# Where the last batch keeps its held tiles, and the order of the last change between layers

## The chip, the cores and the metric

The kernel runs on one core of a Trainium2 chip. The metric is the device time of one execution in microseconds (us); three executions of the kernel before gave 3567.22, 3568.37 and 3571.44 us, median 3568.37 us. The core's engines are TensorE (PE, matmuls; its weight loads are listed apart as PEld), VectorE (DVE), ScalarE (ACT), GpSimd (POOL), and SyncE (SP), which here does nothing but issue DMAs. Each engine takes its instructions in the order in which the kernel writes them, and waits on the others by semaphores.

## The reference

Two layers over 8 batches of 2048 nodes with 256 features, in fp32. Layer 0 is attention in chunks of 256 keys, each chunk with a softmax of its own, with two layer norms behind it; layer 1 is graph attention with an `elu`, and again a layer norm.

```
# layer 0, heads of 64 features
scores = clip(einsum("bhnd,bhjcd->bhnjc", q, kc) / 8, -10, 10)
scores = where(mask == 0, -10, scores)
attn   = softmax(scores, axis=-1)              # over each chunk of 256 keys
ctx    = einsum("bhnjc,bhjcd->bhnd", attn, vc) # sums the 8 chunks
x1     = layernorm(x + layernorm(ctx @ Wo.T + bo + x) * gamma + beta)
...
# layer 1
Wh     = x1 @ W
e      = leaky_relu(s_src[i] + s_dst[j], 0.2)  # masked by adj
h_out  = elu(softmax_j(e) @ Wh)
x      = layernorm(x1 + h_out)
```

## The kernel before

**Layer 0** of a batch goes in 64 slots, two to a pair, so 32 pairs. A slot is one group of 512 query nodes, one pair of heads and one chunk of keys. For each pair PE writes four score tiles (`unit`, line 424) into PSUM, DVE masks and clips each into an SBUF tile `pr` of 128x1024 (`evict`, line 441), ACT takes the exponential in place (`exps`, line 464), and PE multiplies two `pr` tiles by the values in each `product` (line 475). Scores of pair p+1 are made while the products of pair p run. PSUM gives them three rooms of two banks (`two_banks`), handed out in turn to score tiles, products and projections alike: the first product of a pair takes the room of the second score tile, the second product that of the third. The `pr` tiles come from the pool `prp` with 6 buffers, four to a pair. So the third `pr` of a pair takes the buffer of the first `pr` of the pair before, which the first product has to have read.

After each product ACT copies the result out (line 482), DVE takes reciprocals (line 492), and POOL multiplies and adds to the sum `acc` (lines 499, 501). Each group of 512 nodes, once its two `acc` are complete, goes through `Between`: `output` (line 628), `add` (639), a first norm, `scale` (645), `shift` (616), `again` (648), a second norm, `finish` (ACT applies it and issues the store to `x1D`), a turn, and `values` (670), which makes the layer 1 inputs `waug` and `sd`. For most groups this is laid over the pairs of the next group by the tables `FIRST_OF` to `NEXT_LAST`.

**Layer 1** of a batch has 128 tiles, 16 for each of 8 units (a half of the nodes and a head). `make` builds a weight tile `e` of 128x1024 on DVE (line 916) from a row, a factor and a mask tile that SP loads; `use` is 32 matmuls on it (line 947). When a unit is done, ACT copies it out (line 969) and `close` finishes it in five steps, each called by `rest`: reciprocals on DVE, a scaling, `exp` and `relu` on ACT (1006, 1007), and a last DVE operation into `h1` (1011). In the last batch alone the scaling is one POOL operation (995), else eight on ACT (1001). `Close` then adds the layer 0 result to a group of `h1`, takes its norm and stores the output; its `add`, `sums`, `squares`, `factors` and `finish` are hung on pairs by tables.

Layer 1 of batch b-1 (`lower`) runs along with layer 0 of batch b, four tiles a pair. In the last batch, b = 7, the last `LATE` = 8 slots (pairs 28 to 31) run without it; 16 tiles of batch 6 are held back for the stretch in which the last group of batch 7 goes through `Between`. The order of that stretch is written out by hand in the list `order` (from line 1387): `M` is a `make`, `U` a `use`, `R` one step of `close`, `early` the second norm and `values` of the group before, `steps` those of the last group, `fs` the factors of layer 1 (`fs[0]` begins with the greatest value over nodes, line 737). Every engine's queue follows this list. Behind it layer 1 of batch 7 runs alone (64 calls of `step`, two tiles each); there every third tile is made by ACT (885, 886) and POOL (887).

Memory around the change: in the first batch only (`spare`) half of the `pr` tiles lie in `h1`. In batch 7 the closings of groups 0 and 1 of batch 6 are spread over pairs 20 to 31 (`CLOSING_EARLY`) and load into `qT[:, 0]` and `qT[:, 1]`. The last group's input is loaded by `load_x` into the pool `blocks` at pair 31 and gets its bias in the list `order`.

Of the kernel before, what the change touches and what calls it, by code (L numbers as in the profile page):

```python
# [8 lines left out]
F32 = mybir.dt.float32  # L9
# [5 lines left out]
ALU = mybir.AluOpType  # L15
# [7 lines left out]
def adj_resnorm_kernel(  # L23
# [49 lines left out]
    FIRST = [sum(BANKS[:m]) for m in range(len(BANKS))]  # L73
    TILES = len(UNITS) * NT
    STEP = TILES // SLOTS
    LATE = 8
    WIDE = max(BANKS)
    AHEAD_E = 5
    AHEAD_P = 8
# [153 lines left out]
    class Masks:  # L233
# [57 lines left out]

        return dram[b, g * CH : (g + 1) * CH, :].rearrange("(t p) f -> p t f", p=P)

    def load_x(b, g, name):
        t = blocks.tile([P, QT, F], F32, tag="xb", name=name)
        at = by_node(x, b, g)
        post((name, b, g), nc.sync.dma_start, lambda k: t[:, k, :], lambda k: at[:, k, :])
        return t
# [105 lines left out]

    where = [(s // QS, s % QS // NK, s % NK) for s in range(SLOTS)]
    slab_of, probs, raws, accs = {}, {}, {}, {}
    spare = [1]

    def load_slab(p):
        q, hp, c = where[2 * p]  # L410
# [22 lines left out]
    def evict(s, u, ps):  # L433
        k = s % 2 * KT + u
        if spare and k >= KT:
            at = (s // 2 % 2 * KT + k - KT) * QT
            pr = h1[:, at : at + QT, :].rearrange("p (k t) f -> p k (t f)", k=2)
        else:
            pr = prp.tile([P, 2, CH], F32, tag="pr", name="pr")
        row = slab_of[s // 2][:, s % 2 * KT + u, :]  # L440
        nc.vector.scalar_tensor_tensor(  # L441
            pr,
            ps,
            -CLIP,
            row.unsqueeze(1).to_broadcast([P, 2, CH]),
            op0=ALU.max,
            op1=ALU.min,
        )
        probs.setdefault(s, []).append(pr)
# [12 lines left out]
    def exps(s, u):  # L462
        pr = probs[s][u]
        nc.scalar.activation(pr, pr, AF.Exp, scale=0.125)  # L464
# [66 lines left out]
    class Norm:  # L531
# [46 lines left out]
                    accum_out=self.mv[:, k, 1:2],  # L578
                )

        def factors(self):
            self.rs = small.tile([P, QT], F32, tag="rs", name="rs_" + self.name, bufs=3)
            self.off = small.tile([P, QT], F32, tag="off", name="off_" + self.name, bufs=3)
            nc.vector.tensor_scalar(self.rs, self.mv[:, :, 1], EPS, None, ALU.add)
            nc.vector.tensor_scalar(self.off, self.mv[:, :, 0], ROOT_F, None, ALU.mult)
            nc.gpsimd.tensor_tensor(self.rs, self.rs, nhalf, ALU.pow)
            nc.gpsimd.tensor_mul(self.off, self.off, self.rs)

# [11 lines left out]
    class Between:  # L600

        def __init__(self, b, g, sd, waug):
            self.b, self.g, self.sd, self.waug = b, g, sd, waug
            self.r = load_x(b, g, "xg")
            self.y = blocks.tile([P, QT, F], F32, tag="y", name="y")

        def bias(self):
# [184 lines left out]
    class Layer1:  # L794
        def __init__(self, b, gd, waug):
            self.b, self.gd, self.waug = b, gd, waug
            self.made = self.used = 0
            self.rows, self.edge, self.e = {}, {}, {}
            self.tail, self.held = [], []
            self.room = ep, "e"  # L800
            self.alone = b == B - 1
            self.masks = {}
            self.begun, self.lifted = 0, {}
# [86 lines left out]
        def make(self):  # L890

            if self.made == TILES:
                return
            k = self.made
            n, j = k // NT, k % NT
            _, h = UNITS[n]
            if j == (1 if self.alone else NT // 2):
                self.load_row(n + 1)
            self.made += 1
            if not self.alone:  # L900
                drip()
                if j == 0:
                    need(("row", self.b, n))
                self.load_edge(k + AHEAD_E)
                pool, tag = self.room
                e = pool.tile([P, WIDE * P], F32, tag=tag, name="e")
                row = self.rows[n]
            else:
                if j == NT // 2:
                    self.lift(n + 1)  # L910
                self.make_ahead(k)
                if self.by_pool(k):
                    return
                e = prp.tile([P, WIDE * P], F32, tag="pr", name="e")
                row = self.lifted[n]
            nc.vector.scalar_tensor_tensor(  # L916
                e,
                row,
                self.gd[:, h, j : j + 1],
                self.mask(k),  # L920
                op0=ALU.max,
                op1=ALU.mult,
            )
            self.e[k] = e

        def use(self):
# [14 lines left out]
                    ]  # L941
            e = self.e.pop(k)

            def products(e, j, tiles):
                for i in tiles:
                    for z in range(2):
                        nc.tensor.matmul(  # L947
                            self.pa[i // QT][z * D : (z + 1) * D, i % QT, :],
                            lhsT=e[:, i * P + z * D : i * P + (z + 1) * D],
                            rhs=self.waug[:, j, h, :],  # L950
                            start=(j == 0 and i % QT == 0),
                            stop=(j == NT - 1 and i % QT == QT - 1),
                            skip_group_check=True,
                        )
# [22 lines left out]
        def close(self, u, raw, pas):  # L977
# [12 lines left out]
                nc.vector.tensor_scalar(dn, raw[:, :, D:D1], 1e-30, None, ALU.max)  # L990
            nc.vector.reciprocal(dn, dn)
            yield 1
            if self.alone:
                v = raw[:, :, :D]
                nc.gpsimd.tensor_mul(v, v, dn.to_broadcast([P, n, D]))  # L995
            for k in range(n):
                if k == n // 2:
                    yield 1
                if not self.alone:
# [142 lines left out]
    for g in range(NCH):  # L1142
# [36 lines left out]
        11: [(3, "factors"), (3, "finish")],  # L1179
    }  # L1180
    CLOSING_EARLY = {
        20: [(0, "load", qT, 0)],
        22: [(0, "add"), (0, "sums")],
        23: [(0, "squares")],
        24: [(1, "load", qT, 2), (0, "factors"), (0, "finish")],
        26: [(1, "add"), (1, "sums")],
        27: [(1, "squares")],
        28: [(1, "factors")],
        31: [(1, "finish")],
    }  # L1190
    CLOSING_ALONE = {
        0: [(2, "load", kT, 2)],
# [21 lines left out]
    for b in range(B):  # L1214
# [9 lines left out]
        for p in range(PAIRS):  # L1224
            s0, s1 = 2 * p, 2 * p + 1
            q, i = p // QP, p % QP
            along = lower if b + 1 < B or s0 < SLOTS - LATE else None
            more = p + 1 < PAIRS
            slow[0] = bool(along) and more
            if not slow[0]:  # L1230
# [15 lines left out]

            ending = b + 1 == B and not more
            if ending:
                last = Between(b, NCH - 1, sd, waug)

            hook(FIRST_OF, {})
            if i == QP - 1 and q > 1:
# [14 lines left out]
            else:  # L1267
# [3 lines left out]
                if not lower and masks.left():  # L1271
                    masks.step()
            if ending:
                lower.make()
            hook(MIDDLE_OF, NEXT_MIDDLE)
            for each in closings:
# [13 lines left out]
            if along:  # L1290
                normalize(s0)
                if more:
                    for us_ps in waiting[1:]:
                        evict(*us_ps[0], us_ps[1])
            elif more:
                evict(*waiting[2][0], waiting[2][1])
                exps(*us[3])
            if i == 0 and q:
                send_context(b, q - 1, 1)
            if i == QP // 2:  # L1300
                send_context(b, q, 0)
            if along:
                if more:
                    exps(*us[2])
                along.rest(1)
                along.use()
                along.make()
                along.use()
                along.make()
                along.use()  # L1310
            elif ending:
                lower.use()
                group.again()
# [73 lines left out]
        else:  # L1387


            lower.room = prp, "pr"  # L1390
            M, U, R = lower.make, lower.use, lambda: lower.rest(1)
            order = [begin, U, U, ctx, early[0], steps[0], steps[1], early[2], steps[2]]
            order += [lambda: group.a.stats(every), before.turn_all, lambda: coming.load_masks(0)]
            order += [group_shift, M, M, U, steps[4], early[5], U, early[6], M]
            order += [steps[5], U, M, M, R, U, M, U, steps[6], R, steps[7], M, M, U, steps[8], R]
            order += [U, steps[9], M, R, M, M, U, U, R, fs[0], M, U, fs[1], M, U, fs[2], lambda: coming.start(fs[4])]
            done = sum(p is U for p in order) + 1, sum(p is M for p in order) + 1
            order += [R, M, U] * (LATE * STEP - done[0])
            assert LATE * STEP - done[0] >= LATE * STEP - 2 - done[1]
        for piece in order:  # L1400
            send()
            piece()
# [67 lines left out]
```

## Time and profile before

| what | value |
|---|---|
| time, median of 3 | 3568.37 us (3567.22 to 3571.44) |
| time of the profiled execution | 3565.6 us |
| its span, first to last instruction | 3563.7 us |
| granted TensorE clock, mean | 0.997 |
| PE busy | 3500.3 us, 98% |
| DVE busy | 3025.5 us, 85% |
| ACT busy | 2308.5 us, 65% |
| POOL busy | 1421.3 us, 40% |
| scores, line 424 | 8192 matmuls, 942.4 us |
| products, line 475 | 30720 matmuls, 980.6 us |
| layer 1 products, line 947 | 32768 matmuls, 1051.6 us |
| `evict`, line 441 | 960 x 1203 ns |
| `exps`, line 464 | 960 x 1054 ns |
| `make`, line 916, from a row in SBUF | 896 x 1334 ns |

Busy times are sums over the whole span. Where PE is busy all the time, an idle other engine costs nothing; where PE has gaps, the question is what it waits for. The page's second part cuts the span into 40 slices of 89 us each with one digit for each engine. The trace also gives an engine's instructions in order of time, each with the idle time ahead of it and what ended it, and the busy time of the engines in any stretch that one names.

### The profile page before, as it was taken

What the parts mean: (1) busy time and instruction counts of PE and PEld (TensorE: products, weight loads), DVE (VectorE), ACT (ScalarE), POOL (GpSimd) and SP (SyncE); (2) the same over time, 40 slices, a digit from 0 to 9 for tenths busy, and PEclk for the clock granted to TensorE, in tenths of its full rate; (3) what the DMA queues carried; (4) which work ended last, traced back from release to release, by engine and by line L of the source; (5) the groups of instructions that cost most, each with busy time, mean ns of one, the idle gap of its engine ahead of it and who ended that gap; (6) DMA issues with size and microseconds to landing.
All of it is one profiled execution on the core that took longest, in us unless ns stands there. A gap on an engine that the chain in (4) does not pass through costs nothing. (4 is left out here: it accounts for less than half of the span.)

```text
span 3563.7 us, 170248 instructions
## 1 busy us (share of the span) xinstructions
PE 3500.3 (98%) x76924; PEld 2607.6 (73%) x76924; DVE 3025.5 (85%) x3640; ACT 2308.5 (65%) x4151; POOL 1421.3 (40%) x1261
## 2 busy tenths in 40 slices
PE   8999999999999999999999999999999999999888
PEld 5666677777777777777777767777677776777677
DVE  5886699987999789996999969999699996999778
ACT  4787456655766666665666656666576665766677
POOL 1555233333443333333343334433343342434467
PEclk9999999999999999999999999999999999999999
DMA  7663333443434434434444434344343434444322
GB/s 178 150 133 79 85 102 102 108 101 100 115 107 109 101 111 114 110 103 91 124 110 112 104 89 123 106 111 102 96 125 109 108 94 103 126 111 114 106 86 68
DMA packets 719271, 385.53 MB, mean 108 GB/s; under 512 B 432976, under 2 KB 678608, under 8 KB 718544
## 3 DMA queue, kind: packets, MB, share of 16 engines
q1 hardware_dynamic: 668544, 340.95, 37.4%
q10 hardware_dynamic: 50000, 33.70, 3.0%
q8 instruction: 601, 9.85, 1.1%
q14 instruction: 126, 1.03, 0.1%
HBM read 317.59 MB, written 56.89 MB: 105 GB/s over the span
## 5 line engine op out<-in xcount | busy, mean ns | idle before, releaser
L464 ACT ACTIVATE pr<-pr 128x1024 f32<-128x1024 f32 x960 | 996.2, 1054 | 433.4 <-DVE pr L441 364.8
L441 DVE SCALAR_TENSOR_TENSOR pr<-ps,slab 128x1024 f32<-128x1024 f32 x960 | 1115.2, 1203 | 95.7 <-PE ps L424 83.1
L916 DVE SCALAR_TENSOR_TENSOR e<-srow,gd,et 128x1024 f32<-128x1024 f32 x896 | 1165.5, 1334 | 5.6 <-DMA srow<-rowD 0.6
L947 PEld LDWEIGHTS pa<-waug,e 128*64 128x64 f32 x32768 | 999.4, 138 | 199.9 <-issue 172.2
L947 PE MATMUL pa<-waug,e 128*64 128x65 f32 x32768 | 1051.6, 223 | 20.5 <-DVE e L916 14.1
L475 PE MATMUL pc<-vaug,pr 128*64 128x65 f32 x30720 | 980.6, 222 | 5.4 <-DVE pr L441 5.1
L499 POOL TENSOR_TENSOR part<-raw,rd 128x512 f32<-128x512 f32 x446 | 474.4, 1064 | 1224.6 <-DVE rd L492 1220.5
L475 PEld LDWEIGHTS pc<-vaug,pr 128*64 128x64 f32 x30720 | 938.0, 138 | 19.5 <-DVE pr L441 16.4
L424 PE MATMUL ps<-qT,kT 64*64 64x512 f32 x8192 | 942.4, 596 | 5.9 <-DVE pr L441 3.3
L424 PEld LDWEIGHTS ps<-qT,kT 64*64 64x64 f32 x8192 | 286.6, 132 | 483.7 <-issue 270.0
L482 ACT COPY raw<-pc 128x520 f32<-128x520 f32 x512 | 303.0, 592 | 492.7 <-PE pc L475 490.0
L501 POOL TENSOR_TENSOR acc<-acc,part 128x512 f32<-128x512 f32 x446 | 584.4, 1310 | 35.0
L492 DVE RECIPROCAL rd<-raw 128x8 f32<-128x8 f32 x512 | 100.3, 196 | 131.3 <-ACT raw L482 124.5
L499 POOL TENSOR_TENSOR acc<-raw,rd 128x512 f32<-128x512 f32 x64 | 66.9, 1046 | 353.0 <-DVE rd L492 353.0
L670 PE MATMUL pw<-w_sb,x1T 128*64 128x264 f32 (+1 forms) x800 | 124.3, 392 | 0.7 <-ACT x1T L336 0.6
L368 PE MATMUL pp<-xT,wk_sb 128*128 128x512 f32 x256 | 118.8, 604 | 2.9 <-DVE xT L324 1.6
L628 PE MATMUL po<-wo_sb,qT 128*64 128x256 f32 (+1 forms) x912 | 121.5, 382 | 0.0
L368 PE MATMUL pp<-xT,wq_sb 128*128 128x512 f32 x256 | 117.4, 598 | 0.0
L1001 ACT ACTIVATE sums<-sums,dn 128x64 f32<-128x64 f32 x448 | 117.1, 335 | 0.4 <-ACT y L591 0.4
L384 PE MATMUL pv<-wv_sb,xT 128*128 128x256 f32 x512 | 116.6, 381 | 0.0
L384 PEld LDWEIGHTS pv<-wv_sb,xT 128*128 128x128 f32 x512 | 95.9, 190 | 20.2 <-issue 7.2
L916 DVE SCALAR_TENSOR_TENSOR e<-rowp,gd,et 128x1024 f32<-128x1024 f32 x86 | 103.8, 1268 | 1.3 <-PE rowp L783 1.3
(151 smaller groups left out, 2514.0 us busy)
## 6 DMA issues: line engine op xcount, KB each, us to landing
et<-edgeD SPq DMA_DIRECT2D x896, 128.0 KB, 2.6
slab<-clipD SPq DMA_DIRECT2D x256, 256.0 KB, 3.7
srow<-rowD SPq DMA_DIRECT2D x252, 128.0 KB, 3.5
xg<-in_x_dram SPq DMA_DIRECT2D x128, 128.0 KB, 3.2
x1D<-y ACTq DMA_DIRECT2D x32, 512.0 KB, 3.0
ctxD<-acc ACTq DMA_DIRECT2D x56, 256.0 KB, 3.7
ctx<-ctxD SPq DMA_DIRECT2D x224, 64.0 KB, 2.9
xp<-in_x_dram SPq DMA_DIRECT2D x224, 64.0 KB, 2.2
```

The source lines that it names most:

```text
L368: nc.tensor.matmul(pps[c], lhsT=w[:, kc, c * P : (c + 1) * P], rhs=st["xT"][:, kc, :], start=(kc == 0), stop=(kc == KC - 1),)
L384: nc.tensor.matmul(pv[:, u, :], lhsT=st["xT"][:, kc, u * P : (u + 1) * P], rhs=wv_sb[:, kc, :], start=(kc == 0), stop=(kc == KC - 1),)
L424: nc.tensor.matmul(ps[z * D : (z + 1) * D, k, :], lhsT=kT[rows, hp, t * P + z * D : t * P + (z + 1) * D], rhs=qT[rows, hp, cols], start=Tr ...
L441: nc.vector.scalar_tensor_tensor(pr, ps, -CLIP, row.unsqueeze(1).to_broadcast([P, 2, CH]), op0=ALU.max, op1=ALU.min,)
L464: nc.scalar.activation(pr, pr, AF.Exp, scale=0.125)
L475: nc.tensor.matmul(pc[z * D : (z + 1) * D, k, to], lhsT=probs[s][u][:, k, i * P + z * D : i * P + (z + 1) * D], rhs=vaug[:, KT * c + u, 2 ...
L482: nc.scalar.copy(raws[s].rearrange("p k i d -> p k (i d)"), pc[:, :, : QT * D1])
L499: engine.tensor_mul(part, raw[:, :, :, :D], rd.to_broadcast([P, 2, QT, D]))
L501: engine.tensor_add(accv, accv, part)
L670: nc.tensor.matmul(pw[z, k, : F + 2 * H], lhsT=self.x1T[:, c, u * P + z.start : u * P + z.stop], rhs=w1_sb[:, c, :], start=(c == 0), stop= ...
L916: nc.vector.scalar_tensor_tensor(e, row, self.gd[:, h, j : j + 1], self.mask(k), op0=ALU.max, op1=ALU.mult,)
L947: nc.tensor.matmul(self.pa[i // QT][z * D : (z + 1) * D, i % QT, :], lhsT=e[:, i * P + z * D : i * P + (z + 1) * D], rhs=self.waug[:, j, h ...
```

## The change

`LATE` goes from 8 to 12, so that layer 1 of batch 6 ends its run alongside after pair 25 and 24 tiles are left for later. Room for more tiles is found in memory that is used up by then:

- from pair 26 on, the third `pr` of each pair lies by turns in `qT[:, 0, :1024]` and in the first quarter of `h1` (`lone`), not in `prp`;
- pairs 27 to 30 each call `rest` and `make` once; the first goes into `ep`, the next three into the second quarter of `h1` and two pieces of `qT` (`extra`); the views `like` and `block` fit row, mask and matmul operand to the shape of the third piece;
- the last group's input goes into `kT[:, 0]`, and its bias is added in pair 31, ahead of that pair's `make`, which now goes into `prp`.

Closings 0 and 1 of batch 6 take pairs 20 to 27 in place of 20 to 31. Units 6 and 7 of batch 6 are scaled by POOL, not by ACT. In the last list, `again` of the group before moves from pair 31 to behind `ctx`; the second norm of that group takes `sums` and `squares` on ACT and `factors` on POOL in place of `stats` on DVE; the list has 23 `U` and 17 `M` in another order, with all `U` ahead of `coming.start`.

```diff
-    LATE = 8
+    LATE = 12
...
-    spare = [1]
+    spare, lone = [1], []
...
             pr = h1[:, at : at + QT, :].rearrange("p (k t) f -> p k (t f)", k=2)
+        elif lone and k == KT:
+            pr = lone[s // 2 % 2]
         else:
...
-        def factors(self):
+        def factors(self, engine=nc.vector):
...
-            nc.vector.tensor_scalar(self.rs, self.mv[:, :, 1], EPS, None, ALU.add)
-            nc.vector.tensor_scalar(self.off, self.mv[:, :, 0], ROOT_F, None, ALU.mult)
+            engine.tensor_scalar(self.rs, self.mv[:, :, 1], EPS, None, ALU.add)
+            engine.tensor_scalar(self.off, self.mv[:, :, 0], ROOT_F, None, ALU.mult)
...
-            self.r = load_x(b, g, "xg")
+            self.r = load_x(b, g, "xg", room)
...
-                e = pool.tile([P, WIDE * P], F32, tag=tag, name="e")
+                if self.extra:
+                    e = self.extra.pop(0)
+                else:
+                    e = pool.tile([P, WIDE * P], F32, tag=tag, name="e")
...
-            if self.alone:
+            by_pool = self.alone or (self.b == B - 2 and u > len(UNITS) - 3)
+            if by_pool:
                 v = raw[:, :, :D]
                 nc.gpsimd.tensor_mul(v, v, dn.to_broadcast([P, n, D]))
...
     CLOSING_EARLY = {
-        20: [(0, "load", qT, 0)],
-        22: [(0, "add"), (0, "sums")],
-        23: [(0, "squares")],
-        24: [(1, "load", qT, 2), (0, "factors"), (0, "finish")],
-        26: [(1, "add"), (1, "sums")],
-        27: [(1, "squares")],
-        28: [(1, "factors")],
-        31: [(1, "finish")],
+        20: [(0, "load", qT, 0), (1, "load", qT, 2)],
+        21: [(0, "add"), (0, "sums")],
+        22: [(1, "add"), (0, "squares")],
+        23: [(0, "factors"), (0, "finish"), (1, "sums")],
+        26: [(1, "squares")],
+        27: [(1, "factors"), (1, "finish")],
     }
...
+            if b + 1 == B and not along:
+
+                lone[:] = [
+                    qT[:, 0, : 2 * CH].rearrange("p (k n) -> p k n", k=2),
+                    h1[:, :QT, :].rearrange("p (k t) f -> p k (t f)", k=2),
+                ]
+                if p == PAIRS - 4:
+                    lower.extra = [
+                        h1[:, QT : 2 * QT, :].rearrange("p t f -> p (t f)"),
+                        qT[:, 1, : 2 * CH],
+                        qT[:, :, 2 * CH : 3 * CH],
+                    ]
...
             if ending:
+                last.bias()
+                lower.room = prp, "pr"
                 lower.make()
...
                 exps(*us[3])
+                if lone and p >= PAIRS - 5:
+                    lower.rest(1)
+                    lower.make()
...
                 lower.use()
-                group.again()
                 normalize(s0, nc.vector)
...
-            lower.room = prp, "pr"
             M, U, R = lower.make, lower.use, lambda: lower.rest(1)
-            order = [begin, U, U, ctx, early[0], steps[0], steps[1], early[2], steps[2]]
-            order += [lambda: group.a.stats(every), before.turn_all, lambda: coming.load_masks(0)]
-            order += [group_shift, M, M, U, steps[4], early[5], U, early[6], M]
-            order += [steps[5], U, M, M, R, U, M, U, steps[6], R, steps[7], M, M, U, steps[8], R]
-            order += [U, steps[9], M, R, M, M, U, U, R, fs[0], M, U, fs[1], M, U, fs[2], lambda: coming.start(fs[4])]
-            done = sum(p is U for p in order) + 1, sum(p is M for p in order) + 1
-            order += [R, M, U] * (LATE * STEP - done[0])
...
+            b2 = lambda: before.b2
+            order = [begin, U, U, U, ctx, before.again, M, lambda: b2().sums(every), U, steps[1], M]
+            order += [steps[2], lambda: group.a.stats(every), lambda: b2().squares(every)]
+            order += [lambda: b2().factors(nc.gpsimd), U, U, U, M, U, M, U, early[2], steps[4]]
+            order += [before.turn_all, lambda: coming.load_masks(0), group_shift, M, U, early[5], early[6]]
+            order += [steps[5], M, U, R, M, U, M, U, R, steps[6], M, U, steps[7], M, U, R, M, U, steps[8]]
+            order += [M, U, steps[9], R, M, U, M, U, R, M, U, fs[0], M, U, fs[1], M, U, fs[2], U]
+            order += [lambda: coming.start(fs[4])]
```

More of the change, by code (lines that the diff above doesn't have):

```diff
@@ L292, in by_node, with load_x @@
         return dram[b, g * CH : (g + 1) * CH, :].rearrange("(t p) f -> p t f", p=P)
-    def load_x(b, g, name):
-        t = blocks.tile([P, QT, F], F32, tag="xb", name=name)
+    def load_x(b, g, name, t=None):
+        if t is None:
+            t = blocks.tile([P, QT, F], F32, tag="xb", name=name)
         at = by_node(x, b, g)
@@ L600, in adj_resnorm_kernel, with __init__ @@
     class Between:
-        def __init__(self, b, g, sd, waug):
+        def __init__(self, b, g, sd, waug, room=None):
             self.b, self.g, self.sd, self.waug = b, g, sd, waug
-            self.r = load_x(b, g, "xg")
+            self.r = load_x(b, g, "xg", room)
             self.y = blocks.tile([P, QT, F], F32, tag="y", name="y")
@@ L799, in __init__ @@
             self.tail, self.held = [], []
-            self.room = ep, "e"
+            self.room, self.extra = (ep, "e"), []
             self.alone = b == B - 1
@@ L915, in make, with like @@
                 row = self.lifted[n]
+            def like(t):
+                return t if len(e.shape) == 2 else t.rearrange("p (c n) -> p c n", c=e.shape[1])
             nc.vector.scalar_tensor_tensor(
                 e,
-                row,
+                like(row),
                 self.gd[:, h, j : j + 1],
-                self.mask(k),
+                like(self.mask(k)),
                 op0=ALU.max,
@@ L942, in use, with block @@
             e = self.e.pop(k)
+            def block(e, i, z):
+                if len(e.shape) == 2:
+                    return e[:, i * P + z * D : i * P + (z + 1) * D]
+                at = i % QT * P + z * D
+                return e[:, i // QT, at : at + D]
             def products(e, j, tiles):
@@ L948, in products @@
                             self.pa[i // QT][z * D : (z + 1) * D, i % QT, :],
-                            lhsT=e[:, i * P + z * D : i * P + (z + 1) * D],
+                            lhsT=block(e, i, z),
                             rhs=self.waug[:, j, h, :],
@@ L998, in close @@
                     yield 1
-                if not self.alone:
+                if not by_pool:
                     v = raw[:, k, :D]
@@ L1248, in adj_resnorm_kernel @@
             if ending:
-                last = Between(b, NCH - 1, sd, waug)
+                room = kT[:, 0, : QT * F].rearrange("p (t f) -> p t f", f=F)
+                last = Between(b, NCH - 1, sd, waug, room)
             hook(FIRST_OF, {})
@@ L1387, in adj_resnorm_kernel @@
         else:
-            lower.room = prp, "pr"
             M, U, R = lower.make, lower.use, lambda: lower.rest(1)
-            order = [begin, U, U, ctx, early[0], steps[0], steps[1], early[2], steps[2]]
-            order += [lambda: group.a.stats(every), before.turn_all, lambda: coming.load_masks(0)]
-            order += [group_shift, M, M, U, steps[4], early[5], U, early[6], M]
-            order += [steps[5], U, M, M, R, U, M, U, steps[6], R, steps[7], M, M, U, steps[8], R]
-            order += [U, steps[9], M, R, M, M, U, U, R, fs[0], M, U, fs[1], M, U, fs[2], lambda: coming.start(fs[4])]
-            done = sum(p is U for p in order) + 1, sum(p is M for p in order) + 1
-            order += [R, M, U] * (LATE * STEP - done[0])
-            assert LATE * STEP - done[0] >= LATE * STEP - 2 - done[1]
+            b2 = lambda: before.b2
[6 more added lines that the diff above has]
+            order += [lambda: coming.start(fs[4])]
+            assert sum(p is U for p in order) + 1 == LATE * STEP
+            assert sum(p is M for p in order) + 2 + 1 + 4 >= LATE * STEP
         for piece in order:
```

## The prediction, made before the changed kernel ran

> **What bounds the kernel now.** I read the page's slices first. PE is the bound: 9 nearly throughout, 98% of the span. It falls to 8 only in the last three slices, and its clock stays at 9.
>
> ```profile
> PE   8999999999999999999999999999999999999888
> PEclk9999999999999999999999999999999999999999
> ```
>
> The matmuls are the same before and after, so the change is worth what it takes from PE's idle time around pair 26 to the start of the lone layer 1. I cut that stretch by PE's timeline, at each pair's first score matmul. Columns: stretch, then for PE, PEld, DVE, ACT and POOL busy us and instructions, granted clock, DMA share, GB/s. The rows are pair 26 (with tiles), pair 28 (without), two parts of the last change, and the start of layer 1 alone.
>
> ```profile
> 3297.38:3311.38 14.00, 13.38 (x308) 9.63 (x304) 13.94 (x15) 9.11 (x18) 4.65 (x4) 1.00 0.34 100
> 3324.93:3333.84 8.91, 7.70 (x162) 5.02 (x161) 5.86 (x9) 8.37 (x18) 3.65 (x5) 1.00 0.47 124
> 3365.11:3376.53 11.42, 6.97 (x45) 4.12 (x45) 8.37 (x25) 3.67 (x6) 4.46 (x4) 0.80 0.71 241
> 3376.53:3387.54 11.01, 11.01 (x193) 8.65 (x193) 10.87 (x20) 5.17 (x12) 2.33 (x3) 0.75 0.21 63
> 3407.20:3424.26 17.06, 11.32 (x320) 11.04 (x320) 8.96 (x10) 16.83 (x24) 11.95 (x6) 0.90 0.38 112
> ```
>
> No engine is full in pair 28 or in the last change: these are waits. The timelines name them (start, us, operation, in brackets the idle time ahead).
>
> ```profile
> 3330.54 1.23 DVE L441 SCALAR_TENSOR_TENSOR pr<-ps,slab 128x1024 f32<-128x1024 f32 x1 [2.10 <-PE pc L475]
> 3331.82 2.09 PE L475 MATMUL pc<-vaug,pr 128*64 128x65 f32 x64 [1.21 <-DVE pr L441]
> ...
> 3365.11 1.09 PE L525 MATMUL pt<-identf,acc 128*128 128x128 f32 x4 [2.87 <-DVE acc L501]
> 3376.53 2.00 PE L947 MATMUL pa<-waug,e 128*64 128x65 f32 x32 [4.45 <-DVE e L916]
> ...
> 3376.57 2.08 ACT L591 ACTIVATE y<-y,off_a,rs_a 128x256 f32<-128x256 f32 x4 [3.45 <-POOL off_a L554]
> ```
>
> The first two rows are one circle: the third eviction waits until the first product frees a `pr` buffer, and the second product waits for that eviction, 1.21 us in each of pairs 28, 29 and 30. In the last change PE waits 2.87 us for `acc` and 4.45 us for a tile whose `make` DVE reached late; the last row shows the norm chain of the last group on ACT. Matmuls after these gaps run cold: `output` takes 4.76 us for 32 where two halves take 3.8, one tile 2.00 where others take 1.0.
>
> **Pairs 20 to 31.** Each tile taken out of pairs 26 and 27 saves PE about 0.96 us (2.87 for three, 0.98 for one), eight 7.6. PE's waits of pairs 26 to 30 add up to 0.49 + 0.29 + 3 x 1.21 + 0.17 = 4.6. I count them as gone: the third `pr` lies in `lone`, and the three others of a pair find six buffers, two pairs' worth. What is late next? PE then needs 7.8 us a pair, plus 1.9 for `output` or `values` in all but pair 28. DVE needs 4 evictions of 1.17, 0.4 of reciprocals and at most 1.25 + 1.24 of a `make` and a turn: 7.6. ACT is nearest: 4 x 1.06 + 2 x 0.59 = 5.4, and in pair 27 both `finish` steps (2 x 2.08 and 0.4 of issuing), 10.0 against PE's 9.7; but these stand behind the copies, and PE has `output` meanwhile. I take no stall there, at most 1.5 (the exponentials behind them, with their copy). Sum: **12.2 us** earlier at the first product of pair 31, which I call T0 (before: 3355.54).
>
> Closings 0 and 1 move `sums`, `squares` and `finish` (2.05, 2.43, 2.08 on ACT) into pairs 21 to 23, up to 4.5 in one pair. Before, pair 22 carried 4.1 and no PE gap followed; pair 24 carried 4.1 and a gap of 0.95 did. So 0, between +2 and -1. SP is passed by the four output stores of closing 1 (2.56 us of issuing) in pair 28, behind `x1t` (4.44), which waits for `x1D`; they land about 13 us after pair 28 starts, and the `make` of pair 29, which writes where they read, stands at 14.7. The `x1t` load ahead of them is wanted at 12.3 and there at 11. This costs nothing with some 1.5 us to spare; without it the `make` waits on DVE with the next pair's evictions behind it, but PE needs those only 3 us later. The last group's load goes earlier, since `kT[:, 0]` is free after pair 27; its four issues (2.40) no longer wait for `xb`.
>
> **T0 to the lone layer 1, in us after T0.** Bias (1.23) comes ahead of pair 31's `make`, `again` (1.23) goes behind `acc`. They cancel, but both share a port with POOL's work on `acc`: `make` there took 2.20. `ctx` starts at about 9.2 (before 9.6); six to seven held tiles now fill PE, one more ahead of `output`, which at full clock ends at 15.0 (before 15.3). Add and statistics (3.2) and POOL's `off_a` bring 20.6 (before 21.0).
>
> Here the new order costs. ACT's `apply` of the last group stands behind `early[2]`, which waits for the group before: its `sums` and `squares` are done by 15, but its four `factors` operations stand on POOL **behind** those of the last group. POOL's rows: four such in the lone layer, and the same power in the last change.
>
> ```profile
> 3451.17 0.24 POOL L551 TENSOR_SCALAR rs_c<-mv_c 128x4 f32<-128x4 f32 x1
> 3451.48 0.23 POOL L552 TENSOR_SCALAR off_c<-mv_c 128x4 f32<-128x4 f32 x1
> 3451.67 1.04 POOL L553 TENSOR_TENSOR rs_c<-rs_c,nhalf 128x4 f32<-128x4 f32 x1
> 3452.79 0.20 POOL L554 TENSOR_TENSOR off_c<-off_c,rs_c 128x4 f32<-128x4 f32 x1
> ...
> 3366.84 2.03 POOL L553 TENSOR_TENSOR rs_b<-rs_b,nhalf 128x4 f32<-128x4 f32 x1 [7.42 <-DVE off_b L552]
> ```
>
> The four take 1.8 us where DVE makes tiles from a PSUM row. Beside a DVE addition of two SBUF tiles the power alone takes 2.03. So the trace gives 1.8 to 2.7. The Trainium skill (SBUF — State Buffer, Who interferes with whom) speaks against this edit: a DVE operation with two SBUF inputs and a GpSimd one that reads SBUF exclude each other for the whole instruction. DVE has two `make`, `shift` and a third `make` there, all of that kind: by the rule each of the four can wait for one, 1.7 + 4 x 1.2 = 6.5 (an estimate). I take 2.7, the row in the same place; the rule would add 3.8.
>
> Then: 20.6 + 2.7 = 23.3; `apply` of the group before 2.08 and its issue 0.42: 25.8; the last group's `apply` ends at **27.9, before at 23.1: 4.8 later**. `scale`, `again`, statistics and POOL take the same 7.1, `apply` 2.1: 37.1 (before 32.3). Turn, copy and `values` follow as before, except that four scalings (1.07 on ACT) no longer stand ahead of the copy, since POOL does them (1.05, the row of line 995): the copy of `sd` ends at 44.4 (before 40.2). `exp` and `relu` of unit 6 come next (1.3), then DVE's last step (0.7), then one more `make` than before (1.23) ahead of `fs[0]`: 47.7 (before 42.0). One `use` more ahead of `coming.start` adds 0.97 where a gap of 0.35 was. ACT can begin its first lone tile at 55.8, when its row is in PSUM; before it stood ready at 49.5 and began at 51.9, since two late `use` came first. So it begins 3.9 later. PE's second gap there (3.12 us) ends with a `make` that stands behind the last step of unit 7. That step now waits for POOL (1.05 behind its fourth lone tile), not for eight ACT scalings (2.01): about 70 where it ended at 67.5. I take **2.5 us** later.
>
> The eight tiles moved in here cost PE 7.6, but lie in its gaps. Their `make` (four of them within the list) are 4 x 1.24 on DVE, and `stats` of 2.0 goes: all but the one ahead of `fs[0]` lies beside the chain. PE still has a gap of about 4.5 us, from the last ready tile (20.5) to the transposes at 25, and a cold stretch after it.
>
> **Sum:** -12.2 + 2.5 = **-9.7 us**. The profiled execution takes 3565.6 (span 3563.7 and 1.9 around it), so 3555.9. The median shown is 2.8 above that one, within the spread of 4.2; on its scale 3568.4 - 9.7 = **3558.7**. Its own range: pairs 10.5 to 13.5, chain +1 to +5, so 3556 to 3563.
>
> **Rivals.**
>
> 1. *The chain isn't longer.* POOL's four end before they are wanted, or the 2.0 us taken from ACT at the start of the lone layer are worth their full length, since ACT is 16.8 of 17.1 busy there. Then -12.2 and up to -2.6 (PE's first gap there): **3555**. For it: that row of the windows. Against: POOL's queue order, and `fs[0]` behind one more `make`.
> 2. *The new rooms don't end the wait of 1.21.* ACT's or DVE's copies (`raw`, `rd`) come too late and pairs 26 and 27 get the gap as well: 5 x 1.21 = 6.1 of the 12.2 stay: **3565**. For it: the gap of 0.95 after ACT's crowded pair 24, and ACT at 10.0 of 9.7 in pair 27. Against: DVE's 2.10 in the row above is released by PE's product, not by ACT.
> 3. *POOL becomes the bound of the last change.* Slower: every POOL operation there waits out a DVE operation: the four 3.8 more, the last group's second power and product 2.4, the scalings of units 6 and 7 at 1.9 in place of 1.05 (1.7), and the 3.8 that I have the start of the lone layer give back (6.3 to 2.5) are not given back, as POOL starts late and is its bound. Together 11.7: **3570**. It decides once these pass 9.7. For it: 2.03 above and the rule. Against: POOL is busy 4.5 of 11.4 us.
> 4. *Not what it says:* a `make` of pairs 28 to 30 waits for its room (a store, an `apply`) and holds evictions back. This would show as DVE idle ahead of line 916's forms; at 3 us a pair it takes 9, so **3568**.
>
> **Chances.** The forecast 0.50, rival 1 0.18, rival 2 0.14, rival 3 0.11, rival 4 0.07. 0.2% is 7.1 us, about what a measurement of this kernel tells from no change: faster means under 3561.2, slower over 3575.5. Of the forecast some 0.42 lie under 3561.2, of rival 1 all, of the others 0.06; slower are half of rival 3's spread and what a late store would do at its worst, 0.10. That gives 0.66, 0.24 and 0.10. The range 3552 to 3570 takes in the forecast, rivals 1 and 2 and about half of 3 and 4.
>
> **What would show it.** Pairs 26 to 30 at 9.7, 9.5, 7.7, 9.7 and 9.4 us with no gap `<-DVE pr`; the gap ahead of `ctx` below 2 us. The four POOL operations of `factors` straight behind the last group's power, and ACT's `apply` of the last group ending 4 to 5 us later after T0 than before. The first lone row 6 us later after T0, PE's gaps behind it together no longer than before. The prediction is wrong if the pairs keep gaps (rival 2), if the distance from T0 to the lone layer grows by more than 9 us (rival 3), or if that distance does not grow (rival 1).

## The result, and the profile after

The changed kernel takes 3561.95 us (median of 22 runs, 3557.83 to 3567.15) against 3567.67 us before (22 runs, 3566.10 to 3571.96); the ratio is 0.9984, with an interval of 0.9977 to 0.9990. That is 5.7 us where 9.7 were forecast. The interval stays clear of 1, so it is faster, and the time is inside the range; but it is not under 3561.2 (0.2%), where the prediction drew its line for faster. The difference alone stands nearer to the 3.6 us that rival 2 left over (9.7 less 6.1) than to the forecast; what tells them apart is the trace. The profiled execution takes 3559.92 us with a span of 3558.1, 5.6 under the span before, close to the difference of the medians.

The slices of the page: of the three 8 at the end the first is now a 9, the last a 7, in part because the slices end earlier with the span; the clock's row is unchanged. Slices of 89 us are too coarse for this change.

```profile
PE   8999999999999999999999999999999999999987
PEclk9999999999999999999999999999999999999999
```

The stretches show more. Columns as before (stretch; PE, PEld, DVE, ACT, POOL busy us; clock; DMA). The rows are pair 26, pair 28, PE's gap in the last change with what follows it, the start of the lone layer, and the stretch behind that.

```profile
3297.95:3307.69 9.74, 9.74 (x180) 6.09 (x177) 6.69 (x8) 9.44 (x19) 4.18 (x4) 1.00 0.56 160
3316.90:3324.37 7.47, 7.47 (x162) 4.93 (x160) 6.78 (x8) 6.97 (x12) 3.82 (x4) 1.00 0.40 111
3362.57:3376.15 13.58, 8.89 (x76) 5.87 (x74) 7.34 (x16) 5.70 (x11) 4.11 (x6) 0.75 0.63 221
3401.30:3416.95 15.65, 9.70 (x320) 9.42 (x320) 9.24 (x11) 14.44 (x15) 12.75 (x7) 1.00 0.34 108
3416.95:3436.82 19.87, 19.87 (x618) 19.73 (x618) 15.92 (x16) 15.94 (x18) 17.99 (x11) 0.91 0.27 83
```

Pair 28 is now PE from end to end (7.47 of 7.47; it was 7.70 of 8.91). The last change still has a gap, and the clock is again down to 0.75. PE's timeline gives the gaps:

```profile
3351.82 0.63 PE L528 MATMUL pt<-identf,acc 128*128 128x128 f32 x4 [1.40 <-DVE acc L504]
...
3367.13 2.80 PE L334 MATMUL pt<-identf,y 128*128 128x128 f32 x8 [4.49 <-ACT y L594]
...
3396.38 1.15 PE L964 MATMUL pa<-waug,e 128*64 128x65 f32 x32 [0.74 <-DVE e L927]
...
3405.77 7.69 PE L964 MATMUL pa<-waug,e 128*64 128x65 f32 x256 [2.45 <-POOL e L890]
3416.95 19.87 PE L964 MATMUL pa<-waug,e 128*64 128x65 f32 x618 [3.50 <-DVE e L927]
```

Before `ctx` PE waits 1.40 in place of 2.87. The gap of 4.45, which a late `make` ended, has become one of 4.49 that ends with ACT's `apply` of the group before. Read off the two timelines, one execution of each kernel, the 5.6 us are made of these:

| stretch | before | after | change | forecast |
|---|---|---|---|---|
| start to pair 26 | 3297.38 | 3297.95 | +0.6 | 0 |
| pair 26 to T0 (first product of pair 31) | 58.16 | 44.84 | -13.3 | -12.2 |
| T0 to the end of PE's second gap in the lone layer | 68.72 | 74.16 | +5.4 | +2.5 |
| from there to the end of the span | 139.4 | 141.2 | +1.7 | 0 |

Single executions differ in the first row by more than is read there. The changed kernel and the nine profiles made from it below have the same work up to pair 26, yet reach it between 3297.13 and 3303.17 us. So its +0.6 cannot be told from 0, and that the spans differ by as much as the medians owes something to luck. The second and third rows do not depend on it.

### The profile page after: what moved, and what is told of

Same layout as the page of the kernel before. It is cut to its first block, busy times and chain, and to the rows that moved or that the text cites. A ratio compares the mean times of both kernels' runs of the same rounds, so it can differ in the third digit from the quotient of the medians.

```text
span 3558.1 us, 170238 instructions
## 1 busy us (share of the span) xinstructions
PE 3499.2 (98%) x76924; PEld 2605.2 (73%) x76924; DVE 3024.2 (85%) x3630; ACT 2308.5 (65%) x4151; POOL 1429.6 (40%) x1265
```

## Experiments

All ratios are to the kernel before, run beside each kernel on the same chip; kernels of different chips are compared through these ratios. The changed kernel stands at 0.9984.

**Only the lone rooms, in the kernel before.**

```diff
+        elif lone and k == KT:
+            pr = lone[s // 2 % 2]
...
+            if b + 1 == B and not along:
+                lone[:] = [qT[:, 0, : 2 * CH] ..., h1[:, :QT, :] ...]
```

> The kernel before with one part of the change: in pairs 28 to 30 the third score tile is evicted into the two lone rooms. Theory (the pr buffer is what the third eviction waits for): the three gaps of 1.21 us ahead of the second product go, pair 31's first product comes 3.6 us earlier, nothing behind it changes, so about 3.6 us less than before (ratio 0.999). Rival (ACT's or DVE's copies are late anyway): the gaps stay or move to the next score tiles, within 1 us of before.

Measured: 3564.73 against 3568.23 us, ratio 0.9990 (0.9981 to 0.9998). From pair 28 to T0 it takes 27.4 us in place of 30.6. PE's timeline has none of the gaps of 1.21; two small ones came instead, ahead of score tiles of pair 29:

```profile
3335.43 1.09 PE L424 MATMUL ps<-qT,kT 64*64 64x512 f32 x8 [0.35 <-ACT raw L484]
3336.86 1.09 PE L424 MATMUL ps<-qT,kT 64*64 64x512 f32 x8 [0.34 <-DVE pr L443]
```

The wait was for the buffer. What is late next is one copy by ACT, as rival 2 had it, and one eviction: 0.69 us together, not 3.6.

**The whole change without the lone rooms.**

```diff
-        elif lone and k == KT:
-            pr = lone[s // 2 % 2]
```

> The changed kernel without the lone rooms: the third score tile is evicted into the pool prp again. Theory: gaps of 1.21 us return in pairs 26 to 30, 5 x 1.21 = 6 us more than the changed kernel, so level with the kernel before (0.9995 to 1.0005 of it). Rival (a held-back layer 1 alone opens the slack): less than 2 us more than the changed kernel.

Measured: 3570.49 us, ratio 1.0005 (0.9996 to 1.0014), 0.0021 or 7.5 us over the changed kernel. Five gaps are back, one to a pair; two of their rows:

```profile
3305.54 2.09 PE L476 MATMUL pc<-vaug,pr 128*64 128x65 f32 x64 [1.21 <-DVE pr L442]
...
3346.79 2.09 PE L476 MATMUL pc<-vaug,pr 128*64 128x65 f32 x64 [1.21 <-DVE pr L442]
```

Pairs 26 to 30 take 51.8 us in place of 44.8. So holding back eight more tiles gains nothing without the rooms: its new order then costs what the tiles bring.

**Factors of the group before ahead of the last group's statistics.** Only POOL's queue changes: the four operations are issued before the last group's power.

```diff
-            order += [steps[2], lambda: group.a.stats(every), lambda: b2().squares(every)]
-            order += [lambda: b2().factors(nc.gpsimd), U, U, U, M, U, M, U, early[2], steps[4]]
+            order += [lambda: b2().squares(every), lambda: b2().factors(nc.gpsimd), steps[2]]
+            order += [lambda: group.a.stats(every), U, U, U, M, U, M, U, early[2], steps[4]]
```

> The changed kernel with one move in the last list: squares and the four POOL operations of factors for the group before stand ahead of add and stats of the last group, so that POOL's queue no longer holds them behind the last group's power. Theory (ACT's apply of the last group is held by this queue order): the last group's apply ends about 6 us earlier after pair 31's first product (22 in place of 28.3), PE's gap of 4.5 us ahead of the transposes shrinks below 1 us, and the time falls by 4 to 7 us under the changed kernel (0.997 of before). Rival 1 (PE's tiles or DVE's makes set the pace behind it): the apply comes earlier, the first lone row does not, less than 1.5 us gained. Rival 2 (POOL's lock): the four take over 4 us wherever they stand, and less than 3 us is gained.

Measured: 3555.74 us, ratio 0.9968 (0.9956 to 0.9980). POOL's timeline, first of the changed kernel, then of this one (the last row in each is the end of the group before's factors, or the last group's power behind them):

```profile
3360.26 2.05 POOL L556 TENSOR_TENSOR rs_a<-rs_a,nhalf 128x4 f32<-128x4 f32 x1 [11.60 <-DVE off_a L555]
3362.39 0.30 POOL L557 TENSOR_TENSOR off_a<-off_a,rs_a 128x4 f32<-128x4 f32 x1
3362.78 1.08 POOL L587 TENSOR_SCALAR rs_b<-mv_b 128x4 f32<-128x4 f32 x1
3363.94 1.11 POOL L588 TENSOR_SCALAR off_b<-mv_b 128x4 f32<-128x4 f32 x1
3365.13 1.04 POOL L589 TENSOR_TENSOR rs_b<-rs_b,nhalf 128x4 f32<-128x4 f32 x1
3366.24 0.20 POOL L590 TENSOR_TENSOR off_b<-off_b,rs_b 128x4 f32<-128x4 f32 x1
```

```profile
3358.73 0.24 POOL L587 TENSOR_SCALAR rs_b<-mv_b 128x4 f32<-128x4 f32 x1 [9.06 <-ACT junk L575]
3359.04 0.23 POOL L588 TENSOR_SCALAR off_b<-mv_b 128x4 f32<-128x4 f32 x1
3359.35 1.04 POOL L589 TENSOR_TENSOR rs_b<-rs_b,nhalf 128x4 f32<-128x4 f32 x1
3360.47 0.20 POOL L590 TENSOR_TENSOR off_b<-off_b,rs_b 128x4 f32<-128x4 f32 x1
3361.27 2.04 POOL L556 TENSOR_TENSOR rs_a<-rs_a,nhalf 128x4 f32<-128x4 f32 x1 [0.60 <-DVE off_a L555]
```

POOL had been idle for 11.60 us when the last group's power came; in the second order the four use that idleness, and take 1.9 us in place of 3.7. ACT's two `apply` operations follow 6.3 us sooner after T0:

```profile
3366.48 2.07 ACT L594 ACTIVATE y<-y,off_b,rs_b 128x256 f32<-128x256 f32 x4 [6.27 <-POOL off_b L590]
...
3369.00 2.07 ACT L594 ACTIVATE y<-y,off_a,rs_a 128x256 f32<-128x256 f32 x4 [0.45 <-ACT y L594]
```

```profile
3361.11 2.08 ACT L594 ACTIVATE y<-y,off_b,rs_b 128x256 f32<-128x256 f32 x4
...
3363.73 2.08 ACT L594 ACTIVATE y<-y,off_a,rs_a 128x256 f32<-128x256 f32 x4 [0.55 <-POOL off_a L557]
```

T0 is 3342.79 in the first and 3343.79 in the second, so the last group's `apply` ends 28.3 and 22.0 us after it. PE's gap of 4.49 is gone; what remains of it is 1.00 ahead of `values`:

```profile
3366.76 3.78 PE L673 MATMUL pw<-w_sb,x1T 128*64 128x264 f32 x32 [1.00 <-ACT x1T L337]
```

The lone row comes 52.3 us after T0 in place of 58.5. This shows the queue order as the cause, and how much it costs: 6.2 us on the chain. The place in the queue costs in two ways: the four start 14.9 us after T0 in place of 20.0, which is 5.1 of it, and they take 1.7 less where DVE does not hold them up (see below). Some 0.4 is lost again, as ACT still copies sums when they are ready.

**The last three makes moved ahead.** In the changed kernel DVE waits 2.85 us for ACT's `relu` of unit 6 with three makes queued behind that wait.

```profile
3390.26 0.69 DVE L1029 SCALAR_TENSOR_TENSOR h<-ee,sums 128x512 f32<-128x512 f32 x1 [2.85 <-ACT sums L1025]
```

```diff
-            order += [M, U, steps[9], R, M, U, M, U, R, M, U, fs[0], M, U, fs[1], M, U, fs[2], U]
+            order += [M, U, steps[9], R, M, U, M, U, M, M, M, R, U, fs[0], U, fs[1], U, fs[2], U]
```

> The changed kernel with the last three makes of the list moved ahead of the last step of unit 6, into the 2.85 us in which DVE waits for ACT there; so no make stands ahead of the greatest value or behind the factors, and the last held tile ahead of the lone layer waits for none. Theory (these makes are in the chain of the lone layer's first row): that row comes 2 to 3 us earlier, and the time falls by as much under the changed kernel. Rival (the values and the copies behind them set the row, not the makes): within 1 us of the changed kernel.

Measured: 3559.53 us, ratio 0.9975 (0.9965 to 0.9985). The row comes 56.9 us after T0 in place of 58.5, 1.6 earlier, less than the 2 to 3 expected: the last tile no longer waits (1.0), but the greatest value starts only 0.5 earlier, since three makes need more (3 x 1.25) than the wait of 2.85 holds. The time is 0.0009, 3.2 us, under the changed kernel. The row accounts for half of it, and 0.9984 lies within this kernel's interval, so the time alone does not show a gain.

**Both moves.**

> Both moves of the last two experiments in one kernel: factors ahead of the last group's statistics, and the last three makes ahead of the last step of unit 6. Theory (both lie in one chain, one after the other): the gains add, about 8 us under the changed kernel, 0.996 of before. Rival (the first move makes PE's tiles the bound, so that the second buys nothing): no more than the first alone, 0.997.

Measured: 3557.56 us, ratio 0.9964 (0.9952 to 0.9977). The row comes 50.7 us after T0, 1.6 sooner than with the first move alone: in the trace the gains add (6.2 + 1.6 = 7.8). In the time the first move alone stood at 0.9968 on another chip. Beside each other on one chip:

> The kernel with factors ahead of the last group's statistics once more, beside the others on one chip. Theory: its row comes 52.3 us after pair 31's first product, 1.6 behind the kernel with both moves, and it is 1 to 2 us slower than that one; rival: level with it, as the medians so far.

> The kernel with both moves once more, on the same chip. Theory: 1 to 2 us under the kernel with the first move alone; rival: level with it.

Measured: 3558.37 us, ratio 0.9974 (0.9966 to 0.9983), for the first move; 3558.17 us, 0.9971 (0.9960 to 0.9982), for both. The rows came at 52.4 and 51.8. That of both moves came 1.1 later than in its first profile, since one POOL operation ahead of the last group's first `apply` (`off_a`, line 557) took 1.45 there and 0.31 in the first. So both moves are no slower, but the second's 1 to 2 us on top of the first cannot be told from none by these times.

**Two held tiles behind the last values, and then the makes between the factors again.** Both are made on the kernel with both moves.

```diff
-            order += [..., M, U, R, M, U, steps[8]]
-            order += [M, U, steps[9], R, M, U, M, U, M, M, M, R, U, fs[0], U, fs[1], U, fs[2], U]
+            order += [..., M, U, R, M, steps[8]]
+            order += [M, steps[9], R, U, U, M, U, M, U, M, M, M, R, U, fs[0], U, fs[1], U, fs[2], U]
```

> As the kernel with both moves, and two of the held tiles that stand between the last turn and the last values go behind the values, where PE waits for the greatest value. Theory (each such tile, 0.98 us, stands in the chain, and PE's gap behind it is free): 2 us less than with both moves, first lone row 2 us earlier after pair 31's first product. Rival (ACT's copies set the distance from turn to values): within 0.7 us.

Measured: 3557.68 us, ratio 0.9967 (0.9957 to 0.9978): nothing gained, and the row stays at 50.7. Yet not for the rival's reason: counted from T0, ACT's last copy did come 1.8 us sooner (the next expectation has 2.7, which is the difference of the start times in the two traces and leaves out that T0 came 1.0 earlier too). DVE is what is late then, as it was already with both moves; ahead of the greatest value it makes eleven tiles without a gap:

```profile
3374.48 13.99 DVE L927 SCALAR_TENSOR_TENSOR e<-srow,gd,et 128x1024 f32<-128x1024 f32 x11
3388.39 0.68 DVE L1029 SCALAR_TENSOR_TENSOR h<-ee,sums 128x512 f32<-128x512 f32 x1
3389.00 0.21 DVE L740 TENSOR_REDUCE top<-sd 128x4 f32<-128x64 f32 x1
```

```diff
-            ... U, M, U, M, M, M, R, U, fs[0], U, fs[1], U, fs[2], U]
+            ... U, M, U, M, R, U, fs[0], M, U, fs[1], M, U, fs[2], U]
```

> As the kernel with both moves and the two late tiles, but with two of the three makes put back between the factors. In the kernel with late tiles DVE made eleven tiles without a gap (13.99 us) ahead of the greatest value, while the values were there 2.7 us earlier. Theory (DVE's makes, not PE's tiles, now hold the greatest value): it comes 2.4 us earlier after pair 31's first product, near 40 in place of 42.5, and the lone row 1 to 2 us earlier, near 49; in time 1 to 2 us, which these rounds may not tell. Rival (ACT's exp and relu of unit 6 hold it): it stays above 42.

Measured: 3556.84 us, ratio 0.9964 (0.9950 to 0.9977). The greatest value comes 40.1 us after T0 in place of 42.5, as expected, but the row at 51.0, not 49: now PE is late. DVE waits for PE's transpose, which stands behind tiles, and PE's last tile waits for its make:

```profile
3389.40 0.28 DVE L744 TENSOR_REDUCE most<-pt 4x1 f32<-4x128 f32 x1 [2.13 <-PE pt L742]
```

Here the theory named only the nearest wait. With both moves made, PE's tiles and DVE's makes are so nearly level there that moving either lets the other set the time.

**Units 6 and 7 scaled by ACT again.**

```diff
-            by_pool = self.alone or (self.b == B - 2 and u > len(UNITS) - 3)
+            by_pool = self.alone
```

> The changed kernel with units 6 and 7 of batch 6 scaled by eight ACT operations again, as before. Theory (at the start of the lone layer ACT is full and POOL waits for it): DVE's last step of unit 7 comes 1 to 2 us later, and the time rises by 1 to 2 us over the changed kernel. Rival (what ACT gains, POOL gives back): within 0.5 us of the changed kernel.

Measured: 3565.94 us, ratio 0.9991 (0.9982 to 1.0000), 0.0007 or 2.5 us over the changed kernel; PE's second gap in the lone layer ends 75.3 us after T0 in place of 74.2. DVE's last step of unit 7 ends 74.0 us after T0 in place of 72.9, so the direction and the size are the theory's in the trace. The intervals hold 1.1 us as well as 2.5, and 0 too.

The kernels with the first move, alone or with others, beat the one before, and 0.9984 lies above each of their intervals. The changed kernel's own interval, 0.9977 to 0.9990, still meets or overlaps all of these, so the trace carries that comparison more than the times do. The best figures are 0.9964, for both moves and for the kernel with makes between the factors; among the four the times decide nothing.

## Why the prediction was right, point by point

The way from T0 on, in us after it (read from the timelines; the first move is the kernel with factors ahead):

| event | before | forecast | after | first move | both |
|---|---|---|---|---|---|
| `ctx` starts on PE | 9.6 | 9.2 | 9.0 | 9.0 | 9.0 |
| last group's first `apply` ends | 23.1 | 27.9 | 28.3 | 22.0 | 22.0 |
| its second `apply` ends | 32.3 | 37.1 | 37.6 | 31.4 | 31.4 |
| greatest value starts | 42.0 | 47.7 | 49.3 | 43.1 | 42.5 |
| lone row in PSUM | 49.6 | 55.8 | 58.5 | 52.3 | 50.7 |
| PE's second gap there ends | 68.7 | 71.2 | 74.2 | 67.9 | 66.3 |

- **Pairs: right.** 13.3 us for 12.2. Pairs 26 to 30 took 9.74, 9.21, 7.47, 9.26 and 9.16 us. The circle through `prp` was the cause (the two experiments on the lone rooms), and ACT's crowded pair 27 made no stall. No `make` of pairs 27 to 30 has idle time ahead of it on DVE: rival 4 is out, and so is rival 2, as no gap is left in these pairs.
- **Closings moved up: 0 taken, +0.5 in PE's gaps.** PE has new gaps of 0.77 in pair 21 and 0.69 in pair 24, and lost that of 0.95 in pair 25. That is within the bounds given; which ACT operation makes each was not tried. The gap in pair 24 stands in all ten profiles of this order (0.68 to 0.72), that in pair 21 varies.
- **The order on POOL: right, and its size too.** `apply` of the last group came 5.2 us later than before, 4.8 forecast. The four operations took 3.7 us where I took 2.7 from the row, and 6.5 was my estimate from the rule of the Trainium skill (SBUF — State Buffer, Who interferes with whom). The two first operations took 1.08 and 1.11 where they take 0.24 alone, as the rule has it; the power behind them took the 1.04 that it takes alone. DVE's rows show why only two of the four waited:

```profile
3362.55 1.22 DVE L619 TENSOR_TENSOR kT<-kT,beta_sb 128x1024 f32<-128x1024 f32 x1
3363.69 1.28 DVE L927 SCALAR_TENSOR_TENSOR e<-srow,gd,et 128x1024 f32<-128x1024 f32 x1
3371.10 1.23 DVE L648 TENSOR_TENSOR y<-y,gamma_sb 128x1024 f32<-128x1024 f32 x1 [6.14 <-ACT y L594]
```

  Each of the two ends 0.1 us behind a DVE operation with two SBUF inputs; then DVE was idle, waiting for the last group's `apply`, and the last two had nothing to wait for. For the first two the rule held; the estimate of 6.5 gave each of the four a DVE operation to wait for. `output` ending 0.8 earlier hid most of my shortfall. That the chain did grow keeps rival 1 out. Rival 3 is nearer than the time tells: the lone row came 9.0 us later after T0 (8.95), at the very limit that the prediction set as its sign. It is out because two of the four waited and not all, and because the start of the lone layer gave back what I had.
- **From the last `apply` to the lone row: the step that was mis-sized.** The prediction put it that turn, copy and `values` "follow as before", except for four scalings less, with one `make` more ahead of `fs[0]`, and that one `use` more ahead of `coming.start` "adds 0.97 where a gap of 0.35 was". That sum is 18.7 us from the second `apply` to the row; it was 17.3 before and 20.9 now. Two terms of about 1.1 each were missing.

  The first lies between the second `apply` and the greatest value: 10.6 forecast, 11.6 measured. The list has two `use` between the last turn and `values` where it had one, which the sum left out. PE's rows, first of the kernel before, then of the changed one with ACT's copy:

```profile
3388.59 1.15 PE L947 MATMUL pa<-waug,e 128*64 128x65 f32 x32
3390.30 2.00 PE L670 MATMUL pw<-w_sb,x1T 128*64 128x264 f32 x16 [0.56 <-ACT x1T L336]
```

```profile
3381.60 2.23 PE L964 MATMUL pa<-waug,e 128*64 128x65 f32 x64
3383.66 1.95 PE L673 MATMUL pw<-w_sb,x1T 128*64 128x264 f32 x16
...
3381.71 1.01 ACT L337 COPY x1T<-pt 128x1024 f32<-128x1024 f32 x1 [1.29 <-PE pt L334]
```

  Before, `values` waited for the copy; now the copy ends 0.9 us ahead of `values`, which starts behind the second tile. So that tile costs 0.9, and the 0.6 credited for the scalings gained 0.1 at most: the copy ends 2.3 us after the second `apply`, before 2.4. The steps behind were 0.3 shorter than forecast. Where the two tiles were moved, `values` begins 2.2 us after the turn and not 3.1, which shows this term; the row gained nothing, since DVE's makes took their place.

  The second lies between the greatest value and the row: 8.1 forecast, 9.2 measured. The `use` ahead of `coming.start` waits for a `make` which DVE reaches only after `fs[1]`: 0.74 on PE, with its own 0.97 (the row at 3396.38 above). Moving the makes takes 1.0 out of this stretch, which shows this term.
- **What the start of the lone layer gives back: right.** From the row to the end of PE's second gap it gave back 3.5 us where I had 3.8 (6.3 less 2.5).
- **The lone layer behind it: 0 taken, +1.7 measured.** In this execution 1.6 of it is the clock (below). Whether the change makes that more or less frequent was not shown.

The sum of the misses is 0.6 - 1.1 + 2.9 + 1.7 = 4.1 us, which is the difference between 9.7 and the 5.6 of the profiled execution.

## What to carry to other kernels

When an operation moves to another engine, its place in that engine's queue can count for more than its duration: four operations of 1.9 us cost 6.2, because they stood behind one that could not start yet while the engine idled, and because DVE held two of them up where they then stood. When tiles are held back to fill a chain of short steps, count how many of them stand between every two steps of the chain on every engine, and put those of one engine where that engine waits anyway. Look for the circle through a buffer first: with eight tiles more held back and no room for the third score tile the whole change gained nothing.

## What the runs showed of the hardware

The clock behind PE's two gaps at the start of the lone layer differs from execution to execution, though the work is the same: the kernel with both moves, profiled twice, had 0.91 behind a second gap of 3.50 and 1.00 behind one of 3.51. In the changed kernel it stayed up behind the first gap (2.45 us) and fell behind the second (3.50); both rows are shown above. The kernel with factors ahead did the opposite. PE's rows of that one:

```profile
3400.55 9.17 PE L964 MATMUL pa<-waug,e 128*64 128x65 f32 x256 [2.46 <-POOL e L890]
3411.74 13.46 PE L964 MATMUL pa<-waug,e 128*64 128x65 f32 x454 [2.02 <-DVE e L927]
```

Stretches right behind the gap in question, first of the kernel with factors ahead (first gap), then of the changed one (second gap); the clock is the number ahead of the last two:

```profile
3400.55:3404.00 3.45, 3.45 (x66) 3.45 (x68) 2.48 (x3) 3.38 (x5) 3.17 (x2) 0.53 0.47 138
```

```profile
3416.95:3420.50 3.55, 3.55 (x74) 3.55 (x76) 3.55 (x4) 3.52 (x4) 2.94 (x3) 0.58 0.01 2
```

About half the clock for some 3.5 us costs 1.5 or 1.6 us. Behind the first gap (256 matmuls in 9.17 us, not 7.69) that comes out of the second, 2.02 in place of 3.50, where PE waits for DVE in any case. The second gap ends 15.67 us after the row, in the changed kernel 15.65, so it is free. Behind the second it is paid: 618 matmuls take 19.87 us where the first move's kernel takes 18.30, the greater part of the 1.7 us of the first table. Over the twelve profiles, in the 19.87 us behind the second gap, the clock was 0.91 in four of the five with a gap of 3.50 or 3.51, 0.85 in one of the three with 3.11 to 3.14, and 1.00 in all four with 1.92 to 2.14. From that gap to the end of the span it is 139.3 to 141.4 us in the seven profiles with 1.00, and 141.2 to 143.3 in the other five.

The Trainium skill (TensorE: Matmul & The Clock Gate, What's actually happening) has the clock fall after an idle window of about 3.4 us, and these windows run free of the kernel's start. That fits gaps near 3.4 that are punished in some executions only, and a cold time of 3.5 us; that a gap of 2.46 or 3.11 can be punished too doesn't follow from it. The changed kernel's 22 runs spread over 9.3 us, those of the kernel before over 5.9. This clock is not all of it: ahead of pair 26, where the work is the same, the profiles already differ by 6 us, and what makes that was not asked.
